# Flamingo block, first attention: the estimate of the reciprocal deviations in PSUM, a Newton step in three instructions, and one rounding ordered behind three scalings

## The chip, the cores and the metric

The kernel runs on one core of a Trainium2 chip. A core has five engines, each with a queue of its own that it works off in order: TensorE (PE, matrix products, written to PSUM), VectorE (DVE), ScalarE (ACT, functions of one operand such as exp), GpSimd (POOL, elementwise work here[...]) and SyncE (SP, which issues transfers).[...] The metric is the time of one execution on the device in microseconds (us).

## The reference, cut to what matters

Four residual steps act on x of shape (16, 128, 256): a first attention, a feed-forward layer, a second attention and a layer of experts. The change touches the first attention alone:

```python
ln_out = _ln(hidden_states, ln_w, ln_b)
q = _fp8_linear_pertensor(ln_out, wq, wq_scale, q_in_scale).reshape(b, s, g, hpg, d)
q = _ln(q, qln_w, qln_b)
k = _fp8_linear_pertensor(ln_out, wk, wk_scale, k_in_scale).reshape(b, s, g, d)
k = _ln(k, kln_w, kln_b)
v = _fp8_linear_pertensor(ln_out, wv, wv_scale, v_in_scale).reshape(b, s, g, d)
core = _gqa(q, k, v).reshape(b, s, nh * d)
...
cat = jnp.concatenate([core, xout], axis=-1)
catq = _div_clamp_fp8(cat, proj_smooth)
return jnp.einsum('bsi,oi->bso', catq, wproj) * (proj_in_scale * proj_w_scale)
```

There are 16 query heads and 8 key heads of 128 numbers. Every head of every token is normalised by its own deviation: 16 + 8 = 24 reciprocal deviations a token. `xout` is the same attention with keys and values from `ctx_2048`. The attention's result is rounded to the 8-bit format e4m3 before the output projection.

## The kernel before, in words

The first attention is worked in 32 units: units 0 to 15 are the self attention of the 16 batch entries (128 tokens each), units 16 to 31 their cross attention. A unit has eight blocks of 512 projected columns: 0 and 1 are keys, 2 to 5 queries, 6 and 7 values. The attention of a unit runs in four steps c, of four query heads each.

One loop over n (L626) issues, in a pipeline written out by hand, one step of several units at once: `do(n, lag, ...)` calls a stage for step n - lag, `once` a stage that a unit has once. The stages are methods of `Unit`:

- `project` (L410, PE) and `evict` (L422, ACT) make a block `raw`; `bn` (L431, DVE) takes its statistics.
- `rstd` (L433) makes the 24 variances `q_var` (L438 to L443, DVE) and calls `rsqrt` (L171): ScalarE estimates the reciprocal root as exp(-0.5 ln v) (L175, L176), and four VectorE instructions (L177 to L180) refine it by one Newton step, r(1.5 - 0.5 v r r), into `q_r`. All tiles lie in SBUF.
- `mult` (L454, POOL) scales the six key and query blocks by `q_r`, each in one instruction; `heads` turns them on PE (L463) and copies them out on ACT with scale and bias (L472) as `kT` and `qT`.
- `scores` (L481, PE) fills one of two PSUM buffers (`ps_sc`), `top` (L489, DVE) takes the maxima, `exp` (L497, ACT) the exponentials, `recip` (L505, DVE) and `divide` (L509, POOL) divide by the sums, `probs` (L517 PE, L519 ACT) turns the result, `values` (L527, PE) multiplies with the values.
- `smooth` (L538, DVE) scales the result out of PSUM; `quant` calls `e4m3` (L209) on every second step: L215, L216, L220 and L221 on DVE make `e_t` and `e_e`, and their difference is the rounded number. That last step is left to `quant_last`, which calls `last` (L227, POOL) and writes `cat`. `output` (L565, PE) multiplies `cat` by the projection's weights. The inputs of a self unit are rounded by the same helper (`xs`, `xx` from `in_y`).

For the unit two ahead, `rstd` and the first scalings are issued in round n = 4u + 6 of unit u, and the second rounding of unit u in round 4u + 7. What each engine's queue holds in the end is decided by a scheduler: it reorders instructions within what the dependencies allow, by a model of their durations. Before the change it sets the second rounding of unit u ahead of the scalings of unit u + 2 in GpSimd's queue in nearly all self units.

## Time and profile before

| | us |
|---|---|
| median of 3 runs | 1542.24 (1539.53 to 1543.59) |
| profiled execution | 1540.11 |
| its span | 1538.2 |
| busy in it: PE, DVE, ACT, POOL | 1388.1, 1052.2, 814.6, 669.5 |
| first attention, self units | about 53 to 480 |
| first attention, cross units | about 480 to 910 |
| the rest (feed-forward, second attention, experts) | 910 to 1538 |

The span is the profiled execution from its first to its last instruction. A busy time is the sum of an engine's instructions, and an instruction that is held while it runs counts as busy for all of that time. Waits are given as "engine tile line <- engine tile line": who stood idle, and whose end released it. A mean granted clock below 1.00 is a TensorE that was not given its full clock all the time. Lines are those of the kernel before.

### The profile page before, as it was taken

How to read it: one execution, taken by the hardware profiler on the slowest of the kernel's cores; microseconds unless marked ns; L12 is line 12 of the kernel's file. 1: busy time of each engine (PE TensorE's matmuls, PEld its weight loads, DVE VectorE, ACT ScalarE, POOL GpSimd, SP SyncE). 2: the span in 40 equal slices, each digit the busy share in tenths (PEclk: the TensorE clock that was granted, in tenths of full speed). 3: DMA queues.
4: the chain of work that ended last, by engine and by line, in shares of the span. 5: the costliest groups of instructions: out<-in, count | busy, mean ns of one | idle time of the engine just before them, and what ended most of it. 6: DMA issues, size and time to landing. Idle time of an engine off the chain costs nothing. (4 is left out here: it accounts for less than half of the span.)

```text
span 1538.2 us, 24640 instructions
## 1 busy us (share of the span) xinstructions
PE 1388.1 (90%) x8612; PEld 1009.7 (66%) x8612; DVE 1052.2 (68%) x2788; ACT 814.6 (53%) x2421; POOL 669.5 (44%) x574
## 2 busy tenths in 40 slices
PE   2778889798897999999999986999999999996998
PEld 1567677677675677777777764555556666664887
DVE  8888878878789777676767765433579797883100
ACT  3656566566556676666666662353355454542121
POOL 4576666666766555556565554120021312111111
PEclk9799999999999999999999998999999999996999
DMA  4300000000013100000000003400210100001662
GB/s 122 112 7 18 28 11 32 15 11 22 11 45 100 44 23 22 11 19 15 18 15 18 8 8 110 141 1 0 83 49 9 50 9 36 9 36 63 194 198 67
DMA packets 51115, 68.67 MB, mean 45 GB/s; under 512 B 5291, under 2 KB 37739, under 8 KB 50992
## 3 DMA queue, kind: packets, MB, share of 16 engines
q1 hardware_dynamic: 36912, 41.31, 9.1%
q10 hardware_dynamic: 11456, 17.63, 3.6%
q0 software_dynamic: 2624, 8.16, 1.5%
q8 instruction: 68, 1.11, 0.3%
q14 instruction: 55, 0.45, 0.1%
HBM read 50.53 MB, written 16.81 MB: 44 GB/s over the span
## 5 line engine op out<-in xcount | busy, mean ns | idle before, releaser
L509 POOL TENSOR_TENSOR e<-e,sums 128x512 f32<-128x512 f32 x128 | 139.7, 1092 | 230.8 <-DVE sums L505 120.8
L497 ACT ACTIVATE e<-ps_sc,mx 128x128 f32<-128x128 f32 x512 | 181.3, 368 | 90.1 <-DVE mx L489 82.7
L454 POOL TENSOR_TENSOR raw<-raw,q_r 128x512 f32<-128x512 f32 x192 | 207.9, 1112 | 34.1 <-DVE q_r L180 33.0
L431 DVE BATCH_NORM_STATS2 q_st<-raw 128x6 f32<-128x128 f32 x768 | 174.1, 279 | 66.9 <-ACT raw L422 66.5
L1020 ACT ACTIVATE e<-ps_sc,mx 128x128 f32<-128x128 f32 x512 | 139.7, 384 | 119.1 <-DVE mx L1011 114.1
L565 PE MATMUL ps_acc<-wp,cat 128*128 128x512 f32 x512 | 160.4, 436 | 17.6 <-POOL cat L227 15.5
L463 PE MATMUL ps_tr<-ident,raw 128*128 128x128 f32 x768 | 121.9, 288 | 46.0 <-POOL raw L454 43.8
L227 POOL TENSOR_TENSOR cat<-e_t,e_e 128x1024 fp32r<-128x1024 bf16 x64 | 136.2, 2128 | 53.7 <-DVE e_t L221 52.1
L481 PE MATMUL ps_sc<-kT,qT 128*128 128x128 f32 x1024 | 140.3, 280 | 15.0 <-ACT qT L472 15.0
L481 PEld LDWEIGHTS ps_sc<-kT,qT 128*128 128x128 f32 x1024 | 131.1, 193 | 33.0 <-ACT qT L472 27.0
L463 PEld LDWEIGHTS ps_tr<-ident,raw 128*128 128x128 f32 x768 | 96.0, 147 | 83.3 <-POOL raw L454 58.2
L519 ACT COPY eT<-ps_tr 128x512 f32<-128x512 f32 x128 | 75.4, 589 | 139.0 <-PE ps_tr L517 138.9
L975 POOL TENSOR_TENSOR kb<-kT,hmask 128x512 f32<-128x512 f32 x32 | 33.6, 1067 | 243.9 <-PE ps_sc L1004 184.6
L565 PEld LDWEIGHTS ps_acc<-wp,cat 128*128 128x128 f32 x512 | 95.9, 194 | 57.4 <-POOL cat L227 22.2
L527 PE MATMUL ps_pv<-eT,vt 128*128 128x256 f32 x512 | 132.1, 379 | 1.0 <-DVE cat_y L538 1.0
L422 ACT COPY raw<-ps_mm 128x512 f32<-128x512 f32 x192 | 113.7, 593 | 27.9 <-PE ps_mm L410 24.8
L527 PEld LDWEIGHTS ps_pv<-eT,vt 128*128 128x128 f32 x512 | 95.9, 189 | 31.2 <-issue 9.0
L538 DVE TENSOR_TENSOR cat_y<-ps_pv,r_sm 128x512 bf16<-128x512 f32 x128 | 87.1, 680 | 39.7 <-PE ps_pv L527 39.5
L472 ACT ACTIVATE qT<-ps_tr,hv 128x512 f32<-128x512 f32 x128 | 100.9, 789 | 21.8 <-PE ps_tr L463 19.8
L497 ACT ACTIVATION_READ_ACCUMULATOR e<-ps_sc,mx 128x1 f32 x512 | 105.3, 206 | 0.0
L489 DVE TENSOR_REDUCE mx<-ps_sc 128x4 f32<-128x512 f32 x128 | 87.2, 681 | 23.6 <-PE ps_sc L481 23.6
L1011 DVE TENSOR_REDUCE mx<-ps_sc 128x8 f32<-128x1024 f32 x64 | 78.2, 1222 | 25.0 <-PE ps_sc L1004 23.4
(228 smaller groups left out, 2807.3 us busy)
## 6 DMA issues: line engine op xcount, KB each, us to landing
w1t<-in_w ACTq DMA_DIRECT2D x8, 1024.0 KB, 5.0
w2t<-in_w ACTq DMA_DIRECT2D x8, 1024.0 KB, 5.6
disp<-empty SPq DMA_DIRECT2D x16, 257.0 KB, 8.5
xe<-disp SPq DMA_DIRECT2D x8, 514.0 KB, 3.6
stage<-in_wprojT SPq DMA_DIRECT2D x16, 256.0 KB, 2.7
xg<-in_x SPq DMA_DIRECT2D x4, 512.0 KB, 3.9
xb<-in_x SPq DMA_DIRECT2D x16, 128.0 KB, 2.1
ctx<-in_ctxT SPq DMA_DIRECT2D x16, 128.0 KB, 2.2
```

Of the source, the lines that this page charges most:

```text
L227: nc.gpsimd.tensor_tensor(dst, t[:, part], e[:, part], ALU.subtract)
L422: nc.scalar.copy(raw.rearrange("p h d -> p (h d)"), pm)
L431: nc.vector.bn_stats(self.st[:, 4 * blk + j, :], self.raws[blk][:, j, :])
L454: nc.gpsimd.tensor_tensor(src, src, self.r[:, 4 * blk : 4 * blk + 4, None].to_broadcast([P, 4, P]), ALU.mult,)
L463: nc.tensor.transpose(pt[:, j, :], src[:, j, :], ident)
L472: nc.scalar.activation(dst, pt, AF.Identity, scale=hv[:, col : col + 1], bias=hv[:, col + 1 : col + 2])
L481: nc.tensor.matmul(pscore[:, j, :], qT[:, j, :], self.kT[:, 2 * c + j // 2, :], start=True, stop=True,)
L497: nc.scalar.activation(e[:, j, :], pscore[:, j, :], AF.Exp, bias=self.mx[:, j : j + 1], accum_out=sums[:, j : j + 1],)
L509: nc.gpsimd.tensor_tensor(e, e, sums[:, :, None].to_broadcast([P, 4, P]), ALU.mult)
L527: nc.tensor.matmul(pv[:, 2 * g : 2 * g + 2, :], self.vt[:, gg * P : (gg + 1) * P], eT[:, 2 * g : 2 * g + 2, :], start=True, stop=True,)
L565: nc.tensor.matmul(self.acc, self.cat[c // 2][:, h % 8, :], wpr[self.cross, c][:, j, :, :], start=(h == 0), stop=(h == 15),)
L1020: nc.scalar.activation(e[:, i, :], s[:, i // NQ, i % NQ, :], AF.Exp, bias=mx[:, i : i + 1])
```

## The change

There are three parts. The first replaces the call of `rsqrt` in `rstd`: the estimate is written to a PSUM tile of 24 columns that takes its turn in the two buffers of the scores, and the Newton step is three instructions that each read the estimate there: a = -0.5 r v, a = r a, r' = (a + 1.5) r. The second adds a helper, `stay_after`, that gives the scheduler an order without a semaphore. The third uses it: the second rounding of unit u is kept behind the scaling of block 2 of unit u + 2 in GpSimd's queue, so behind the scalings of both key blocks and of the first query block.

```diff
@@ -99,6 +99,16 @@
             reason=reason,
         )
 
+    def stay_after(ins, other):
+
+        tc.add_manual_dep(
+            ins.ins, other.ins.name,
+            mybir.DependencyInfo(
+                mybir.DependencyClass.NoSync, mybir.DependencyReason.DATA
+            ),
+            reason="the other is awaited",
+        )
+
     def kpn(ap):
         return ap.rearrange("(k p) n -> p k n", p=P)
 
@@ -220,11 +230,13 @@
         nc.vector.tensor_scalar(e, e, 2.0**-6, 24.0, ALU.max, ALU.mult)
         nc.vector.tensor_tensor(t, y, e, ALU.add)
 
-        def last():
+        def last(other=None):
             at = 0
             for dst in dsts:
                 part = slice(at, at + dst.shape[1])
-                nc.gpsimd.tensor_tensor(dst, t[:, part], e[:, part], ALU.subtract)
+                ins = nc.gpsimd.tensor_tensor(dst, t[:, part], e[:, part], ALU.subtract)
+                if other is not None:
+                    stay_after(ins, other)
                 at += dst.shape[1]
 
         return last
@@ -441,7 +453,15 @@
                     var, st[:, :, 2], P * EPS, st[:, :, 5], ALU.add, ALU.add
                 )
                 nc.vector.scalar_tensor_tensor(var, var, 1.0 / P, dif, ALU.mult, ALU.add)
-                self.r = rsqrt(small, var, 24, "q", 2)
+
+                a = small.tile([P, 24], F32, tag="q_a", name="q_a", bufs=2)
+                est = ps_sc([P, 24])
+                self.r = small.tile([P, 24], F32, tag="q_r", name="q_r", bufs=2)
+                nc.scalar.activation(a, var, AF.Ln)
+                nc.scalar.activation(est, a, AF.Exp, scale=-0.5)
+                nc.vector.scalar_tensor_tensor(a, est, -0.5, var, ALU.mult, ALU.mult)
+                nc.vector.tensor_tensor(a, est, a, ALU.mult)
+                nc.vector.scalar_tensor_tensor(self.r, a, 1.5, est, ALU.add, ALU.mult)
 
             def mult_q(self, c):
                 self.mult(c + 2)
@@ -451,10 +471,12 @@
 
             def mult(self, blk):
                 src = self.raws[blk]
-                nc.gpsimd.tensor_tensor(
+                ins = nc.gpsimd.tensor_tensor(
                     src, src, self.r[:, 4 * blk : 4 * blk + 4, None].to_broadcast([P, 4, P]),
                     ALU.mult,
                 )
+                if blk == 2:
+                    self.scaled = ins
 
             def heads(self, blk):
                 src = self.raws.pop(blk)
@@ -551,8 +573,11 @@
                 self.cat[c // 2] = cat
 
             def quant_last(self, c):
-                if c % 2 == 1:
+                if c == 1:
                     self.clast()
+                elif c == 3:
+                    b = units.index(self) + 2
+                    self.clast(units[b].scaled if b < NU else None)
 
             def output(self, c):
                 if c == 0:
```

## The prediction

> **What bounds the kernel now.** I read the busy time by stretch first, because shares over the whole span mix stages. Columns: stretch, length, busy time (instructions) of TensorE, its weight loads, VectorE, ScalarE and GpSimd, then granted clock, DMA share, GB/s.

> ```profile
> 53.00:480.00 427.00, 365.40 (x2034) 302.75 (x2032) 355.40 (x986) 263.26 (x808) 284.02 (x229) 0.96 0.10 30
> 480.00:910.00 430.00, 418.38 (x2172) 311.48 (x2172) 315.46 (x907) 279.39 (x843) 249.64 (x198) 1.00 0.07 20
> ```

> The first row is the self half of the first attention (16 units), the second the cross half. In the cross half TensorE is busy 418 of 430 us: it is the bound, and a faster reciprocal deviation can give almost nothing there. In the self half it idles 62 of 427 us. For what? The table of waits, TensorE alone, 60 to 480 us (total, times, longest):

> ```profile
> PE ps_tr L463 <- POOL raw L454: 41.2, 27, 3.8
> PE ps_sc L481 <- ACT qT L472: 12.5, 15, 1.7
> PE ps_acc L565 <- POOL cat L227: 2.7, 1, 2.7
> ```

> Two thirds of the idle time is one wait: the transposes (L463) want blocks that GpSimd scales (L454), once a unit. The timeline of one unit tells why (start, length, engine, line; in brackets the idle time before and who ended it):

> ```profile
> 330.09 1.37 POOL L509 TENSOR_TENSOR e<-e,sums 128x512 f32<-128x512 f32 x1 [1.75 <-DVE sums L505]
> 330.48 1.02 DVE L177 TENSOR_TENSOR q_a<-q_r 128x24 f32<-128x24 f32 x1
> 331.43 2.12 POOL L227 TENSOR_TENSOR cat<-e_t,e_e 128x1024 fp32r<-128x1024 bf16 x1
> 331.54 2.05 DVE L178 TENSOR_TENSOR q_a<-q_a,q_var 128x24 f32<-128x24 f32 x1
> 333.83 0.18 DVE L180 TENSOR_TENSOR q_r<-q_r,q_a 128x24 f32<-128x24 f32 x1
> 334.10 6.03 POOL L454 TENSOR_TENSOR raw<-raw,q_r 128x512 f32<-128x512 f32 x6 [0.56 <-DVE q_r L180]
> 335.19 0.66 PE L463 MATMUL ps_tr<-ident,raw 128*128 128x128 f32 x4 [2.48 <-POOL raw L454]
> 336.19 0.66 PE L463 MATMUL ps_tr<-ident,raw 128*128 128x128 f32 x4 [0.34 <-POOL raw L454]
> 337.61 0.60 PE L463 MATMUL ps_tr<-ident,raw 128*128 128x128 f32 x4
> 337.97 1.17 PE L565 MATMUL ps_acc<-wp,cat 128*128 128x512 f32 x4
> ```

> L178 multiplies 24 columns, yet takes 2.05 us and ends where the rounding `cat` on GpSimd ends (331.43 + 2.12 = 333.55). L177 likewise ends with the division L509. Unhindered they are short (ns, min/median/max over all 32 units):

> ```profile
> L177 DVE TENSOR_TENSOR q_a<-q_r x32: 168/183/1023, 55.6 to 903.1; 128x24 f32<-128x24 f32 x32
> L178 DVE TENSOR_TENSOR q_a<-q_a,q_var x32: 166/908/2111, 55.9 to 903.3; 128x24 f32<-128x24 f32 x32
> L538 DVE TENSOR_TENSOR cat_y<-ps_pv,r_sm x128: 655/678/694, 74.7 to 938.9; 128x512 bf16<-128x512 f32 x128
> L489 DVE TENSOR_REDUCE mx<-ps_sc x128: 655/679/693, 65.7 to 930.1; 128x4 f32<-128x512 f32 x128
> ```

> L538 and L489 read PSUM, and in 128 executions each never vary by more than 39 ns. So a VectorE instruction with both inputs in SBUF is held while GpSimd works; one with an input in PSUM is not. From the third to the fifteenth unit (starts 107 to 446 us) L178 is held behind the rounding 13 times, for 1.6 to 2.1 us, and the waits of TensorE before L463 that follow are 3.83, 2.49, 3.00, 2.49, 2.48, 2.48, 3.01, 2.49, 2.48, 2.48, 2.48, 2.64 and 2.65 us: 35.0 us.

> **The change, part by part.** *The estimate in PSUM.* ScalarE's L176 (median 0.22 us) writes 24 columns to PSUM instead of SBUF; no row of before has ScalarE writing PSUM, so it is bounded by 0.21 us (the row's least) and the 0.37 us of the 128-column exponential L497, and I take the row it replaces, 0.22. Both ScalarE instructions keep their places in its order. *The Newton step.* Four instructions (0.18 + 0.18 + 0.17 + 0.18 unhindered, 0.21 from start to start) become three, each with one input in PSUM, none held. I take 3 x 0.21 = 0.63 us plus 0.08 to GpSimd's start. [...]

> *The score buffer.* The estimate takes a turn in the two PSUM buffers of the scores. In the shown unit it is needed from about 329.8 to 331.1. The score tile after it in the program (fourth block) must then wait for the exponentials of the third, which ended at 336.1; its matmuls came at 339.4, so 3.3 us of slack hides this. If the slack went, TensorE would stand by that much.

> *The rounding behind the scaling.* The order of GpSimd's instructions in the built program is now division, three scalings, rounding, three scalings; TensorE's order around it is unchanged in nearly every unit (eight transposes, four projections, four transposes, four output matmuls). Shown unit: GpSimd is free at 331.46, the deviations are ready at 330.48 + 0.63 = 331.11, so scaling starts at 331.5 instead of 334.10. TensorE, free at 332.71, finds block 0 scaled and starts there instead of at 335.19. But the rounding now runs behind three scalings of 1.005 us each, from 334.54 to 336.66, and the output matmuls L565, which stand behind the transposes in TensorE's queue, read it. Without it they would start at 335.4; they wait until 336.72. Before it was 337.97. The unit gains **1.25 us, not 2.5**: half of the wait moves from L463 to L565. Everything behind L565 shifts by the gain. The other three scalings and the next division end at 340.8, where they ended at 341.1, so they delay nobody.

> *The sum.* The same working (scaling starts at the later of GpSimd free and L177's start + 0.74; L565 at that + 5.2, which is 3 x 1.005 + 2.12 and two hand-overs) for the 13 units, by the start of L454 before: 136, 222, 249, 334, 361 gain 1.25 each (6.2); 107 gains 2.3, 193 1.8, 306 1.8, 388 2.1, 417 1.5, 446 1.9 (11.4; in these units the granted clock was 0.94 or 0.95, not 1.00, and the matmuls from L463 to L565 ran slower). At 164 and 277 the built order puts two statistics and L489 between the three instructions, so the deviations come about 0.9 us later: 0.9 and 0.6 (1.5). Together **19 us**. The first two units and the hand-over to the cross half (477 to 500 us, where weights are split too and TensorE's order does change) I put at 0, with 3 us either way.

> *The cross half.* GpSimd's rounding there waits for e_t (697.56 in the unit at 692.79) with 0.7 us idle before it; scaling that starts 1.2 us sooner, with one more block ahead of it, still lets it start at 697.56. L565 follows at 700.13, 0.45 us after the rounding: no change. VectorE's saving of about 1.3 us a unit, and the missing instruction, lie beside a TensorE busy 97%: nothing. After 910 us nothing differs.

> The profiled execution took 1540.1 us (span 1538.2 and 1.9 around it); 1540.1 - 19 = 1521. The median of the runs is 2.1 us above it, so **1523 us** on the median's scale.

> **The rivals.** *A, the whole wait comes back.* If L565 is not held by the rounding (were the rounding shorter, or TensorE fed with other work), TensorE's own path gives 2.6 to 3.7 us a unit, 38 us in 13 units: about 1506. For it: 41.2 us of wait. Against: 2.12 us of rounding behind 3.0 us of scaling, read directly. *B, only half of the change works.* The two parts remove the same wait: with the rounding moved, L178 would no longer be held by it even in SBUF. If PSUM operands don't free the three instructions from the division L509, scaling starts at about 332.2 and L565 at 337.4: 0.6 us a unit, 8 us: about 1534. L538's even times speak against it. *C, slower: the rounding comes late.* Since it now stands behind three scalings, its end is start of scaling + 5.2 us, and L565 loses when scaling starts after 337.97 - 5.2 = 332.8, that is 1.25 us later than I compute. One place could do it: the estimate stuck on ScalarE behind L472 and L419, which themselves wait for TensorE. If the deviations came as late as now (334.1), L565 would start at 339.3 and each of 13 units lose 1.3 us: about 1559; halfway, 1550. Against: ScalarE ended the estimate at 330.04, and VectorE was then busy with L221 anyway.

> **How the numbers follow.** Forecast 0.60 (gain of 12 to 25 us, 1517 to 1530), A 0.15, B or a similar remnant 0.15, C 0.10. A measurement of this kernel tells a change from none at about 0.3%, 4.6 us; the runs of before lie within 0.2%. Faster: all of the forecast and A, 0.12 of B, 0.87; same: 0.03 of B and 0.02 of C, 0.05; slower: 0.08. The range takes in A's end and most of B, 1506 to 1535, and leaves C out.

> **What would show it.** In the profile of the changed kernel the three instructions should each take about 0.2 us in all units; TensorE's wait for raw in the self half should fall from 41 us to under 10; a wait of L565 for cat of about 1.3 us a unit should appear, 15 to 18 us in all; TensorE's clock in the self half should read 0.98 or more; the cross half should keep its 26.5 us a unit (L454 started at 692.79 and 719.31). The prediction is wrong if the L565 wait is missing (A), if the three instructions still stretch (B), or if the estimate on ScalarE starts more than a microsecond after L175 (C).

## The result, and the profile after

The change takes **1515.79 us** (median of 5 runs, 1515.08 to 1518.37), the kernel before beside it on the same chip 1540.71 us (5 runs, 1536.95 to 1543.59): a ratio of 0.984, 95% interval 0.982 to 0.986, so 24.5 us saved. The forecast was 1523 us, its range 1506 to 1535. The profiled execution took 1515.79 us, its span is 1514.1 (before 1538.2).

Where the 24.1 us of the span went is seen in the same two stretches, their bounds moved with the work and rounded (columns as in the prediction: stretch, length, busy time of TensorE, weight loads, VectorE, ScalarE, GpSimd, granted clock):

```profile
53.00:458.00 405.00, 358.49 (x2033) 295.89 (x2031) 325.81 (x970) 258.37 (x799) 283.67 (x228) 0.98 0.10 32
458.00:885.00 427.00, 417.39 (x2169) 311.29 (x2169) 313.79 (x891) 279.53 (x846) 252.61 (x199) 1.00 0.07 20
```

The self half took 427 us and takes 405; TensorE's idle time in it fell from 62 to 47 us and its clock rose from 0.96 to 0.98. The cross half keeps 26.48 us a unit (26.52 before). VectorE lost 30 us of busy time in the self half, nearly all of it time in which it had been held.

The table of waits, TensorE alone, 60 to 455 us (total, times, longest):

```profile
PE ps_acc L590 <- POOL cat L237: 14.7, 13, 2.0
PE ps_sc L503 <- ACT qT L494: 14.6, 15, 2.0
PE ps_tr L485 <- POOL raw L474: 11.7, 22, 1.8
```

The lines moved: the transposes L463 are L485, the scaling L454 is L474, the rounding L227 is L237, the output matmuls L565 are L590, the scores L481 are L503. So the wait for the scaled blocks fell from 41.2 to 11.7 us, and a wait for `cat` that hardly existed (2.7 us, once) is now there in 13 units, 14.7 us. The instructions of the estimate and the Newton step, by the tile `q_a` (ns, min/median/max over all 32 units):

```profile
L461 ACT ACTIVATE ps_sc<-q_a x32: 182/194/249, 54.8 to 879.4; 128x24 f32<-128x24 f32 x32
L462 DVE SCALAR_TENSOR_TENSOR q_a<-ps_sc,q_var x32: 168/176/184, 55.6 to 879.6; 128x24 f32<-128x24 f32 x32
L463 DVE TENSOR_TENSOR q_a<-ps_sc,q_a x32: 160/182/183, 55.9 to 879.8; 128x24 f32<-128x24 f32 x32
L464 DVE SCALAR_TENSOR_TENSOR q_r<-q_a,ps_sc x32: 165/170/180, 56.8 to 880.5; 128x24 f32<-128x24 f32 x32
```

None of the three is ever held: their longest are 184, 183 and 180 ns, where L177 and L178 reached 1023 and 2111. The timeline of the unit that answers to the one shown before (start, length):

```profile
316.79 1.37 POOL L531 TENSOR_TENSOR e<-e,sums 128x512 f32<-128x512 f32 x1 [1.75 <-DVE sums L527]
316.57 0.69 DVE L231 TENSOR_TENSOR e_t<-cat_y,e_e 128x1024 bf16<-128x1024 bf16 x1
317.18 0.17 DVE L462 SCALAR_TENSOR_TENSOR q_a<-ps_sc,q_var 128x24 f32<-128x24 f32 x1
317.39 0.18 DVE L463 TENSOR_TENSOR q_a<-ps_sc,q_a 128x24 f32<-128x24 f32 x1
317.61 0.18 DVE L464 SCALAR_TENSOR_TENSOR q_r<-q_a,ps_sc 128x24 f32<-128x24 f32 x1
318.13 3.03 POOL L474 TENSOR_TENSOR raw<-raw,q_r 128x512 f32<-128x512 f32 x3
321.12 2.13 POOL L237 TENSOR_TENSOR cat<-e_t,e_e 128x1024 fp32r<-128x1024 bf16 x1
323.22 3.03 POOL L474 TENSOR_TENSOR raw<-raw,q_r 128x512 f32<-128x512 f32 x3
319.24 0.63 PE L485 MATMUL ps_tr<-ident,raw 128*128 128x128 f32 x4
...
321.64 0.60 PE L485 MATMUL ps_tr<-ident,raw 128*128 128x128 f32 x4
323.31 1.20 PE L590 MATMUL ps_acc<-wp,cat 128*128 128x512 f32 x4 [1.06 <-POOL cat L237]
```

The three instructions of the Newton step run inside the division (316.79 to 318.16); scaling starts as it ends; the first transposes, at 319.24, show no wait; and the output matmuls stand 1.06 us until the rounding ends at 323.25. Steady units (those at full clock) took 27.08 us and take 25.73.

### The profile page after: what moved, and what is told of

The parts are those of the page before. It is cut to its first block, busy times and chain, and to the rows that moved or that the text cites. A ratio compares the mean times of both kernels' runs of the same rounds, so it can differ in the third digit from the quotient of the medians.

```text
span 1514.1 us, 24690 instructions
## 1 busy us (share of the span) xinstructions
PE 1381.9 (91%) x8612; PEld 1004.0 (66%) x8612; DVE 1022.1 (68%) x2756; ACT 810.6 (54%) x2421; POOL 672.7 (44%) x574
## 5 line engine op out<-in xcount | busy, mean ns | idle before, releaser
L531 POOL TENSOR_TENSOR e<-e,sums 128x512 f32<-128x512 f32 x128 | 139.7, 1091 | 226.7 <-DVE sums L527 108.8
L474 POOL TENSOR_TENSOR raw<-raw,q_r 128x512 f32<-128x512 f32 x192 | 211.9, 1129 | 19.8 <-DVE q_r L464 18.9
L590 PE MATMUL ps_acc<-wp,cat 128*128 128x512 f32 x512 | 159.4, 433 | 27.4 <-POOL cat L237 26.9
L237 POOL TENSOR_TENSOR cat<-e_t,e_e 128x1024 fp32r<-128x1024 bf16 x64 | 136.3, 2129 | 47.4 <-DVE e_t L231 47.4
L503 PE MATMUL ps_sc<-kT,qT 128*128 128x128 f32 x1024 | 140.4, 280 | 17.1 <-ACT qT L494 17.1
L503 PEld LDWEIGHTS ps_sc<-kT,qT 128*128 128x128 f32 x1024 | 131.0, 193 | 35.4 <-ACT qT L494 28.7
L590 PEld LDWEIGHTS ps_acc<-wp,cat 128*128 128x128 f32 x512 | 94.7, 191 | 69.6 <-POOL cat L237 35.9
L485 PE MATMUL ps_tr<-ident,raw 128*128 128x128 f32 x768 | 115.4, 277 | 16.1 <-POOL raw L474 14.2
L434 ACT COPY raw<-ps_mm 128x512 f32<-128x512 f32 x192 | 114.0, 594 | 26.6 <-PE ps_mm L422 24.1
L485 PEld LDWEIGHTS ps_tr<-ident,raw 128*128 128x128 f32 x768 | 91.9, 142 | 50.4 <-POOL raw L474 23.5
L549 PEld LDWEIGHTS ps_pv<-eT,vt 128*128 128x128 f32 x512 | 96.5, 190 | 31.5 <-issue 11.4
L560 DVE TENSOR_TENSOR cat_y<-ps_pv,r_sm 128x512 bf16<-128x512 f32 x128 | 86.9, 679 | 39.9 <-PE ps_pv L549 39.7
L511 DVE TENSOR_REDUCE mx<-ps_sc 128x4 f32<-128x512 f32 x128 | 87.1, 680 | 36.5 <-PE ps_sc L503 35.9
```

The source lines that it names most:

```text
L237: ins = nc.gpsimd.tensor_tensor(dst, t[:, part], e[:, part], ALU.subtract)
L434: nc.scalar.copy(raw.rearrange("p h d -> p (h d)"), pm)
L474: ins = nc.gpsimd.tensor_tensor(src, src, self.r[:, 4 * blk : 4 * blk + 4, None].to_broadcast([P, 4, P]), ALU.mult,)
L485: nc.tensor.transpose(pt[:, j, :], src[:, j, :], ident)
L503: nc.tensor.matmul(pscore[:, j, :], qT[:, j, :], self.kT[:, 2 * c + j // 2, :], start=True, stop=True,)
L531: nc.gpsimd.tensor_tensor(e, e, sums[:, :, None].to_broadcast([P, 4, P]), ALU.mult)
```

## The experiments

All kernels below start from the changed kernel and were timed against the kernel before on the same chip (medians of 9 runs, 1544.04 us in the first set, 1543.96 in the second). A gain is the ratio's distance from 1 times that median; the change itself is 24.5 by its own ratio. The intervals are worth 2 to 3 us either way. A gain of a single unit is read from the profiled execution, and units are named by the start of their scaling before, in us. Line numbers differ a little from kernel to kernel; the tiles are the same.

| kernel | us | ratio (95% interval) | gain, us |
|---|---|---|---|
| the change | 1515.79 | 0.984 (0.982 to 0.986) | 24.5 |
| e1: PSUM and three instructions, no order | 1528.36 | 0.9905 (0.989 to 0.992) | 14.7 |
| e2: order alone | 1529.58 | 0.9906 (0.9891 to 0.9921) | 14.5 |
| e3: order, three instructions in SBUF | 1537.23 | 0.9955 (0.9941 to 0.9968) | 7 |
| e4: the change, rounding in halves | 1504.75 | 0.9749 (0.9735 to 0.9762) | 39 |
| e5: SBUF in self units, PSUM in cross units | 1524.32 | 0.9883 (0.9866 to 0.9899) | 18 |
| e6: the change, rounding done twice | 1580.31 | 1.024 (1.0225 to 1.0255) | -37 |

**e1, the Newton step without the order.** Is the rounding's place needed?

```diff
                 elif c == 3:
-                    b = units.index(self) + 2
-                    self.clast(units[b].scaled if b < NU else None)
+                    self.clast()
```

> The estimate in PSUM and the three instructions as in the change, but without the order on GpSimd: the built program has the rounding ahead of all six scalings again. Theory (two parts remove one wait, and the rounding must get out of the way of both VectorE and GpSimd's own queue): the three instructions take 0.17 us each, but scaling still starts only when the rounding ends, 0.5 us sooner than before in each of 13 units; with the 2 us that the first units gained, about 8 us: 1533. TensorE's wait for raw in the self half stays near 33 us. Rival (the saved VectorE time is what counts): close to the changed kernel, 1516 to 1519.

It gave 1528.36 us. The timeline of the steady unit:

```profile
321.54 2.12 POOL L237 TENSOR_TENSOR cat<-e_t,e_e 128x1024 fp32r<-128x1024 bf16 x1
323.62 6.03 POOL L474 TENSOR_TENSOR raw<-raw,q_r 128x512 f32<-128x512 f32 x6
324.71 0.66 PE L485 MATMUL ps_tr<-ident,raw 128*128 128x128 f32 x4 [1.89 <-POOL raw L474]
...
327.50 1.17 PE L589 MATMUL ps_acc<-wp,cat 128*128 128x512 f32 x4
```

The deviations are ready early here too (the three instructions take 0.16 to 0.18 us in all units), but the rounding stands ahead of the scalings in GpSimd's queue, so these start when it ends; the transposes wait 1.89 us instead of 2.48, and the output matmuls don't wait. The steady unit takes 26.49 us, 0.59 less than before, as the theory had it (0.5); TensorE's wait for `raw` in the self half stays at 29.4 us (33 expected). The whole gained more than the theory's 8, and the rest is not in the steady units: 2.0 us come from the first two units (the theory counted them), 1.3 to 1.8 from each of five units out of the thirteen (those that start at 107, 136, 193, 306 and 446 us before), while two (249 and 388) gain nothing and run at a clock of 0.94. What that clock has to do with it is plainer in e2 and in the last section.

**e2, the order without PSUM**, four instructions in SBUF as before.

```diff
-                est = ps_sc([P, 24])
...
-                nc.vector.scalar_tensor_tensor(self.r, a, 1.5, est, ALU.add, ALU.mult)
+                self.r = rsqrt(small, var, 24, "q", 2)
```

> The order on GpSimd alone; the estimate in SBUF and four instructions as before. Theory: L178 is no longer held by the rounding, but the first of the four is still held by the division in five of 13 units, and the fourth costs 0.2 us: scaling starts 0.7 us later than in the change there and 0.2 us later elsewhere: 14 us of gain, 1527. Rival (the order does it all): 1516. Rival (PSUM does it all): 1541.

It gave 1529.58 us. The timeline of a steady unit:

```profile
324.04 1.37 POOL L523 TENSOR_TENSOR e<-e,sums 128x512 f32<-128x512 f32 x1 [1.75 <-DVE sums L519]
326.17 3.04 POOL L466 TENSOR_TENSOR raw<-raw,q_r 128x512 f32<-128x512 f32 x3 [0.76 <-DVE q_r L190]
324.43 1.02 DVE L187 TENSOR_TENSOR q_a<-q_r 128x24 f32<-128x24 f32 x1
325.48 0.18 DVE L188 TENSOR_TENSOR q_a<-q_a,q_var 128x24 f32<-128x24 f32 x1
...
325.91 0.18 DVE L190 TENSOR_TENSOR q_r<-q_r,q_a 128x24 f32<-128x24 f32 x1
```

L187 (L177 before) is still held until the division ends at 325.41. L188 (L178 before) takes 0.18 us: with the rounding gone from this place, nothing runs on GpSimd that could hold it. GpSimd now stands 0.76 us with nothing to do until the deviations are there. The steady unit takes 26.54 us. That is 0.54 us less than before, and the theory's price; the surplus lies in other units. Before, and e2, the two units at 388 and 417 us before, by stretch:

```profile
388.26:416.62 28.36, 24.82 (x138) 20.87 (x138) 22.36 (x61) 16.43 (x51) 18.75 (x16) 0.94 0.05 15
416.62:445.67 29.05, 25.13 (x138) 20.93 (x138) 22.46 (x61) 16.80 (x52) 18.76 (x16) 0.94 0.14 40
```

```profile
379.27:406.11 26.84, 23.93 (x141) 19.89 (x139) 20.42 (x61) 16.55 (x52) 18.72 (x15) 1.00 0.05 16
406.11:432.98 26.87, 23.81 (x140) 19.79 (x138) 20.54 (x61) 16.59 (x52) 18.73 (x16) 1.00 0.09 26
```

Their granted clock was 0.94 and is 1.00, TensorE's busy time is about 1 us less for the same work, and they gain 1.5 and 2.2 us instead of 0.5. With the units at 107, 193 and 306 (2.1, 1.6 and 1.7, also from 0.94 to 1.00) five units gain 9 us.

So either part alone keeps the rounding from holding L178, but each leaves the scalings waiting for something else: in e1 for the rounding ahead of them in the queue, in e2 for the first of the four instructions, which the division holds (in six of the 13 units; the theory said five). In a steady unit the parts therefore more than add: 0.59 and 0.54 us alone, 1.35 together. The totals look the other way, 14.7 and 14.5 alone, 29 in sum, against 24.5 together. One thing that is counted twice in the 29 is the clock: the units at 193 and 306, at 0.94 before, gain 1.6 and 1.7 us in e1, the same in e2, and 2.4 each in the change. How much of the difference this makes isn't shown, and with three intervals of 2 to 3 us it is hardly clear of the noise.

**e3, the three instructions with the estimate in SBUF**, order kept: is it PSUM, or the missing instruction?

```diff
-                est = ps_sc([P, 24])
+                est = small.tile([P, 24], F32, tag="q_e", name="q_e", bufs=2)
```

> The change with one thing undone: the estimate lies in SBUF, still three instructions, same order. Theory: the first of the three is held by the division in five of 13 units (0.4 us each), else as in the change, and without the gain of the first units: 17 us of gain, 1524. If where the estimate lies makes no difference: 1516, and no instruction of the three above 0.3 us in any self unit.

It gave 1537.23 us, a miss for both. The self half went as the theory said: 17.3 us gained at the fifteenth unit, and a steady unit of 26.34 us, between e2's 26.54 and the change's 25.73. But the cross half gave most of it back: 27.2 us a unit instead of 26.5. A timeline of a cross unit of e3:

```profile
677.92 1.06 POOL L531 TENSOR_TENSOR e<-e,sums 128x512 f32<-128x512 f32 x1 [3.42 <-PE ps_pv L549]
679.79 5.99 POOL L474 TENSOR_TENSOR raw<-raw,q_r 128x512 f32<-128x512 f32 x5 [0.81 <-DVE q_r L464]
678.12 0.91 DVE L463 TENSOR_TENSOR q_a<-q_e,q_a 128x24 f32<-128x24 f32 x1
...
680.12 1.15 DVE L226 TENSOR_SCALAR e_e<-cat_y 128x1024 uint16<-128x1024 uint16 x1
...
681.30 1.15 DVE L230 TENSOR_SCALAR e_e<-e_e 128x1024 bf16<-128x1024 bf16 x1
682.48 1.41 DVE L231 TENSOR_TENSOR e_t<-cat_y,e_e 128x1024 bf16<-128x1024 bf16 x1
683.81 0.68 DVE L511 TENSOR_REDUCE mx<-ps_sc 128x4 f32<-128x512 f32 x1
...
687.38 0.63 PE L485 MATMUL ps_tr<-ident,raw 128*128 128x128 f32 x4 [0.74 <-ACT kT L494]
```

L463 (the second of the three) is held until the division L531 ends and takes 0.91 us instead of 0.18; everything behind it on VectorE is late by 0.7 us. The scalings start just ahead of L226, L230 and L231 (L216, L220 and L221 before), and each of these three, with tiles in SBUF, is held by one scaling (free, they take 0.43, 0.43 and 0.69 us, their medians in the change). So the maxima L511 start late, ScalarE's exponentials with them, and the copy `kT` behind these is late for TensorE. The waits of TensorE in the cross half, 620 to 880 us, of e3 and of the change:

```profile
PE ps_tr L485 <- ACT kT L494: 8.2, 10, 1.0
```

```profile
PE ps_tr L485 <- ACT kT L494: 0.5, 2, 0.2
```

In the change the same three instructions are held as long (1.15, 1.15 and 1.41 us, from 669.04), but the row starts some 0.8 us sooner, and nobody waits. In e2 the deviations come later still, but there scaling starts behind L226, which is free and takes 0.43 us: counted from the start of the division, the deviations are ready after 1.04 us in the change, 1.80 in e3 and 2.26 in e2.

**e5, SBUF in the self units, PSUM in the cross units**, to see whether e3's loss is the cross half's alone.

```diff
-                est = ps_sc([P, 24])
+                est = (
+                    ps_sc([P, 24]) if self.cross
+                    else small.tile([P, 24], F32, tag="q_e", name="q_e", bufs=2)
+                )
```

> As e3_order_sbuf_three, but only the 16 self units keep the estimate in SBUF; the cross units have it in PSUM again. Theory (e3 lost 0.7 us a unit in the cross half, because L463 held by the division made the maxima L511 late there): the self half gains about 16.5 us as in e3 and the cross half gives none of it back, 1526 to 1528 on the scale of a kernel before at 1544; L511's end leaves the eviction of kT in time, and TensorE's wait for kT in the cross half falls from 8 us in ten units to under 2. Rival (the loss has another cause, such as three instructions with no PSUM at all): 1537, unchanged.

It gave 1524.32 us, a little under the theory's range, and the rival falls: by the start of the scalings the gain is 18.7 us in the fifteenth unit and 18.8 in the last cross unit, and TensorE's wait for `kT` in the cross half is 0.7 us. This splits the change in a steady unit: the order alone 0.54 us (27.08 to 26.54, e2), one instruction less 0.20 more (26.34, e5), the estimate in PSUM 0.61 more (25.73, the change), since the first of the three is no longer held by the division. In the totals the steps are 14.5, 3.5 and 6.5 us, but they are less sure: 2.1 us of e5's gain lie in the first two units, where e3, with self units written alike, gained 0.6. In the cross units PSUM is worth nothing against before, and some 10 us against three instructions in SBUF (26.45 against 27.2 us in each of 13 units).

**e4, the rounding in two halves**, in self and cross units, to test what the prediction said of the new wait: that the output matmuls wait for the length of the rounding. A half holds four heads, and each output matmul reads one head, so the first four need the first half only.

```diff
-                    [cat.rearrange("p h s -> p (h s)")],
+                    [cat.rearrange("p h s -> p (h s)")] if c == 1 else
+                    [cat[:, 4 * i : 4 * i + 4, :].rearrange("p h s -> p (h s)") for i in range(2)],
```

> The change, with every second rounding done as two instructions of 512 columns, both behind the three scalings. The first output matmuls need only the first half. Theory (after the change the rounding sets the end of each self unit's stall): the wait of L565 for cat, 14.7 us in 13 waits, falls to under 4 us, 0.95 us a unit less, 12 us in all: 1504. Rival (TensorE loses that time elsewhere, since the scalings set the pace): 1514 to 1519, the extra instruction costing GpSimd 0.24 us a unit.

It gave 1504.75 us, 14 us under the change by the two ratios, and is the fastest of all. TensorE's waits in its self half, and the timeline of a steady unit:

```profile
PE ps_tr L485 <- POOL raw L474: 13.6, 24, 1.8
PE ps_acc L591 <- POOL cat L237: 2.6, 3, 2.0
```

```profile
313.45 3.03 POOL L474 TENSOR_TENSOR raw<-raw,q_r 128x512 f32<-128x512 f32 x3
316.44 2.27 POOL L237 TENSOR_TENSOR cat<-e_t,e_e 128x512 fp32r<-128x512 bf16 x2
316.97 0.60 PE L485 MATMUL ps_tr<-ident,raw 128*128 128x128 f32 x4
317.65 1.20 PE L591 MATMUL ps_acc<-wp,cat 128*128 128x512 f32 x4
```

The output matmuls start right behind the transposes, while the second half is still being rounded. The wait for `cat` fell from 14.7 to 2.6 us, and the steady unit from 25.73 to 24.77. Of the 14 us, 9.7 lie in the thirteen units by the start of their output matmuls (the theory put 12 there): most gain 0.9 to 1.0 us, three next to nothing. Another 4.3 came in the last cross unit (39.9 us from its scalings to the last output matmul, in the change 44.2), which the theory didn't name and no run explains. The second instruction costs GpSimd 0.14 us (2.27 against 2.13).

**e6, the second rounding done twice in the self units** (the same numbers are written again), to make the suspected wait larger.

```diff
-                    self.clast(units[b].scaled if b < NU else None)
+                    for _ in range(1 if self.cross or b >= B else 2):
+                        self.clast(units[b].scaled if b < NU else None)
```

> The change, with the second rounding of self units 0 to 13 done twice; the built program puts one scaling between the two. The output matmuls wait for the second. Theory (the rounding behind the scalings sets when L565 starts): L565 starts 3.1 us later in 13 units, 2.12 for the second rounding and 1.0 for the scaling between; less in the two units where the built order of TensorE moves four transposes ahead of it: 35 us slower than the change, 1551 on the scale of a kernel before at 1541, so slower than the kernel before. Rival (there is slack behind the scalings): within 8 us of the change.

It gave 1580.31 us, far over both. The wait itself grew about as expected, from 14.7 to 49.1 us in 13 units (in the built order one scaling stands between the two roundings, and they wait for it too). But the units also ran at a granted clock of 0.89 to 0.95, as in this one, whose output matmuls took 2.08 us instead of 1.20 after the gap:

```profile
323.80:354.90 31.10, 25.25 (x135) 21.03 (x135) 19.44 (x61) 16.70 (x52) 21.05 (x16) 0.89 0.04 13
```

```profile
332.05 2.08 PE L591 MATMUL ps_acc<-wp,cat 128*128 128x512 f32 x4 [4.11 <-POOL cat L237]
```

The kernel is some 62 us slower than the change. Of these, 56 are lost by the scalings of the fifteenth unit, and 34 of the 56 are the waits. As an estimate from the rows, the clock makes up the rest: at a mean of 0.93 from 104 to 479 us it lacks 26 us, at 0.99 in the same units of the change (103.5 to 423 us) about 3. That is argued, not separated: no run has the wait without the clock. The cross units keep 26.46 us.

## Why the prediction was right

*What bounds the kernel.* Right: of the 24.1 us, 22.6 lie in the first fifteen units of the self half, and the wait of the transposes is what shrank there, as the three rows of waits show.

*Both inputs in SBUF.* Right: "a VectorE instruction with both inputs in SBUF is held while GpSimd works; one with an input in PSUM is not". In the change all three lie inside a division and take 0.17 to 0.18 us; in e2, with SBUF inputs at the same place, the first is held (1.02 us), and in e5 the longest of the three in SBUF are 1.02, 0.60 and 0.47 us, in PSUM 0.18. Rival B, that PSUM operands don't free them, falls. What the sentence leaves out is who came first: in the unit shown after the change, L231 has two inputs in SBUF, began 0.22 us before the division and kept its 0.69 us, while the division took 1.37 us (1.03 at the least). That L231 held it is read from these rows, not tested.

*The price of the three instructions.* Right. With a PSUM operand they cost 0.21 us each from start to start (317.18, 317.39, 317.61), as those in SBUF do (e2: 325.48 to 325.91 over two). The estimate's write to PSUM took 0.19 us (median of 32), below the 0.22 that was taken and the 0.21 that was the lower bound. The turn in the score buffers cost nothing, as predicted: among TensorE's waits in the self half there is none of the scores for an exponential.

*"Half of the wait moves from L463 to L565."* Right, and the core of the forecast: scaling started right behind the division, the output matmuls followed 5.18 us later (323.31 - 318.13; 5.2 was predicted), and 13 units wait 14.7 us for `cat` (15 to 18 predicted). The steady unit gained 1.35 us (27.08 - 25.73) against 1.25. Rival A, the whole wait, falls by that row; e4 shows that it was no limit of TensorE, but the length of the rounding in one piece.

*The sum.* Step by step by the start of the output matmuls, the 13 units gained 20.5 us where 19 were predicted: 1.35 in most steady units; 2.2 and 2.8 in the units at 388 and 446 (2.1 and 1.9 predicted); 1.5 and 1.2 in those at 107 and 193 (2.3 and 1.8), where the prediction took the full clock for granted and the change still has 3.4 us at a clock of 0.50 (105.6 to 109.0 and 184.1 to 187.5); 1.1 and 0.8 in the two with the statistics between (0.9 and 0.6). **The term that was mis-sized is the first units and the hand-over**, put at 0 with 3 us either way: the first two units gave 2.1 us, and what follows the last of the 13 another 1.5. That is 3.6 of the 5.1 us between 19 and the span's 24.1; the other 1.5 is in the 13 units.

*"The two parts remove the same wait."* Half right. With the rounding moved, L178 is indeed free in SBUF too (e2), and 0.6 us a unit for one part alone is what the steady units show (0.59 and 0.54). But the parts don't stand in for each other: the steady unit gains 1.35 us with both. And 8 us for one part was too small (14.7 and 14.5): it left out that units at 0.94 of the clock come back to full clock when the wait shortens, though the prediction counted this where both parts are made.

*The cross half: nothing.* Right for the change (26.48 us a unit), but the reason was incomplete. "A TensorE busy 97%" hides VectorE's work only as far as the chain from `e_t` over the maxima and exponentials to `kT` allows. In e3 deviations that come 0.76 us later than the change's cost 0.69 us a unit against before; in e2 they come 1.2 us later and cost nothing (26.51), because L226 then runs ahead of the scalings. So it is not lateness alone that costs, but which VectorE instructions the scalings meet. The prediction gave no price for that.

*Rival C.* ScalarE's estimate was not stuck and none of the 13 units lost; e6 shows what lay on that side: a rounding that comes 3 us later makes the kernel slower than before.

**Open:** the 2 us of the first two units appear in the change, e1 and e5 (2.1, 2.0 and 2.1), hardly in e2 and e3 (0.0 and 0.6). No part of the change explains this, since e3 and e5 have self units written alike; the clock goes with it. TensorE's was 0.50 from 61.2 to 68.0 us before, just as long in e2 (from 61.0) and half as long in e3 (62.0 to 65.4), and 1.00 there in the change, e1 and e5. It is not the whole: e4 has 0.50 from 62.3 to 65.7 and gained 1.9. The units with the statistics between take 28.3 to 28.4 us in the change and in e1, e3, e4 and e5; no run touched them.

## What to carry to other kernels

Price each part of an edit alone and both together, and by a steady unit rather than by the total: here each part alone left more than half of the gain behind, while the totals, with a clock that comes back only once (0.94 to 1.00), looked as if one part could partly replace the other. Follow what is moved to the next reader in the queue: a step that is ordered out of one consumer's way stands in another's, and its length in one piece is then the price; cutting it to the grain at which it is read gave back most of that (14 us here). A small VectorE instruction on the path, with long GpSimd instructions beside it, is worth keeping a PSUM operand for (here at most 0.18 us with one, up to 2.11 us without). An engine at 97% covers another engine's work only within the slack of the chain between them (e3's cross half lost 0.69 us a unit beside it): look at that chain before counting a cost as hidden.

## What the runs showed of the hardware, unexpected

```profile
358.16:361.57 3.41, 1.63 (x8) 1.04 (x6) 3.31 (x5) 0.59 (x1) 2.86 (x3) 1.00 0.00 0
361.57:364.98 3.41, 2.37 (x15) 1.91 (x16) 1.69 (x7) 3.04 (x11) 3.41 (x4) 1.00 0.00 0
385.47:388.88 3.41, 1.40 (x7) 0.86 (x5) 3.31 (x6) 0.59 (x1) 2.86 (x3) 1.00 0.00 0
388.88:392.29 3.41, 2.93 (x11) 2.46 (x12) 1.46 (x6) 3.07 (x10) 3.41 (x5) 0.50 0.00 0
362.27 0.66 PE L463 MATMUL ps_tr<-ident,raw 128*128 128x128 f32 x4 [2.48 <-POOL raw L454]
389.36 2.11 PE L463 MATMUL ps_tr<-ident,raw 128*128 128x128 f32 x8 [2.48 <-POOL raw L454]
```

With 1.78 us idle in one stretch (3.41 - 1.63) the next ran at full clock; with 2.01 it ran at half. Between 65 and 480 us the eight traces have 918 stretches at full clock: all 32 with over 1.92 us idle were followed by half clock, none of the 857 with under 1.68, and 12 of the 29 between. So a unit at 0.94 is one with 3.41 of its 28 us at half clock, and a gap of 2.48 us (before) or 1.89 us (e1) brings it or not by where it falls in the raster; e1's units at 249 and 388, which gained nothing, were caught so. The change's gap of 1.06 us in a steady unit, taken alone, is below the 1.68 us under which half clock never followed. More than 1.92 of 3.41 us idle, little more than half of a stretch, was enough every time.
- VectorE's instructions with one tensor as input were held by GpSimd as well: L226 and L230, 1024 columns of 2 bytes, take 1.15 us beside a scaling and 0.43 us (the median of each in the change) otherwise.
- GpSimd paid little for an instruction more: two roundings of 512 columns took 2.27 us, one of 1024 took 2.13.
